# A written-out order of five engines set anew with every DMA landing counted, and one subtraction moved from GpSimd to VectorE

## The chip, the cores and the metric

The kernel runs on one core of one Trainium2 chip. The metric is the time of one execution on the device in microseconds, the median of several runs. The core has five engines with a queue of instructions each: TensorE (PE in the profile; its weight loads are PEld), VectorE (DVE), ScalarE (ACT), GpSimd (POOL) and SyncE (SP, which here only issues DMAs). An engine works its queue strictly in order; between engines there are semaphores.

## The reference

An attention block on 32 items, x and y (called ctx_2048) of 256 channels by 1024 columns each, all in fp32. Cut to its core:

```python
x_q = einsum('oc,bcn->bno', w_qk, y);  x_k = einsum('oc,bcn->bon', w_qk, x)
x_v = einsum('oc,bcn->bon', w_v, x) + b_v[None, :, None]
energy = einsum('bnc,bcm->bnm', x_q, x_k)               # 1024 x 1024
attention = softmax(energy, axis=-1)
attention = attention / (1e-07 + attention.sum(axis=1, keepdims=True))
x_r = einsum('bcn,bnm->bcm', x_v, attention)
return x + relu(einsum('oc,bcn->bon', w_t, x - x_r) + b_t[None, :, None])
```

## The kernel before

**Numbers.** Each fp32 operand of a matmul is kept as two fp32r forms, a high one (a rounded copy, made by ScalarE) and a low one (operand minus high form, made mostly by GpSimd). A product is three matmuls of 128x512: high by high, high by low, low by high. Products of 2x2 blocks are made with seven block products instead of eight (Strassen's scheme in Winograd's form), at the price of sums and differences of blocks on VectorE and GpSimd, and of reading partial results out of the banks.

**Words.** A word is one small step of one item, recorded on one engine. A table of words per stage of the program fixes the order: FIRST (item 0), STEADY (a loop body, run for items 1 to 29) and LAST. A plus in front of a word means the next item, a minus the one before. The function `do` goes through a table and calls each word; the class `InOrder` (line 62, the line that the profile gives for nearly everything) makes each of PE, DVE, ACT and POOL keep exactly this order. DMAs of SP are not in `InOrder`: their order among themselves is chosen by the framework that records the program. It also gives each DMA of SP one of eight semaphores in turn.

The words that matter here, for item b:

- `E0P1` to `E3P7`: products of the energies, four pairs of row tiles, accumulated in banks 0 to 3. `E.r.` (ACT) and `E.c..` (DVE) read and combine the banks; the latter also find the row minimum. `exp`, `ri` (reciprocal of the row sum), `h`, `l`, `sum`: exponential, high form, low form and column sums of a row tile.
- `A` + row tile, c, h: attention products, into banks 4 to 7 (c = 0: 4 and 5; c = 1: 6 and 7), with the value tiles `uf` as weights: row tiles 0 to 3 use the first half of `uf`, 4 to 7 the second.
- `xl0`, `xl1`: low forms of x, 512 and 1024 columns. `xT1` to `xT4` (POOL) are differences of x blocks, `xTh`, `xTl` their high and low forms. The same for y: `ys`, `yh`, `yl`, `ysh`, `ysl`.
- `uP`, `xP`, `kP`: products of x with folded weights: u (the values, turned), x (the part of the result without attention) and k (the keys). `kc`, `kT`, `kh`, `kl`, `kTh`, `kTl` make the key blocks and their forms (`kT3`, `kT2` and `kT4` on DVE, `kT1` on POOL).
- `ur`, `uc`: u out of the banks; `ud1` to `ud4` store it to `uspace` in DRAM; `ul0`, `ul1` (four DMAs each) load it back into `turned`; `ut` (DVE) turns it, `uh` (ACT) and `uL` (POOL) make its two forms in `uf`.
- `xr1` to `xr7` (ACT): x parts out of the banks; `xd` store them to `xspace` and `xmspace`. `xr5`, `xr6`, `xr7` write the buffers of `rs` that `ud4`, `ud2`, `ud3` read.
- The end of an item: `cols`, `inv`, `turn` (DVE: column sums, inverse), `div1`, `div0` (DVE: banks 6, 7 and banks 4, 5 into `z`), `join` (a DMA of POOL adds `xspace` to `z`), `more` (a DMA of POOL adds `xmspace`), `pos` (ACT: relu), `add` (a DMA of POOL adds x), `st` (SP stores the result). join, more, pos, add and st of one half of `z` each need the landing of the one before.
- `ldx`, `ldy`: loads of x and y, which share two buffers (`raws`).

So each period of STEADY holds work of three items, and PE has 81 products (243 matmuls) in it.

Of the kernel before, what the change touches and what calls it, by code (L numbers as in the profile page):

```python
# [17 lines left out]
def kernel(  # L18
# [900 lines left out]


    FIRST = """
        xh1 Fxh0 ys03 Fxl0 Fxl1 Sgram Swt Sgh0 ys01 Scorner ldy1 Stp ys02 Sbvw FHH0 Swtc
        FHL0 ys04 Ssq Sgraw Sgh1 Sgl Sbias yh00 yh01 Fyh Gh22 Svh FLH0 FHH1 Svl ysh0
        FLH1 FHL1 yh11 kh11 Fraw22 yl01 ysl0 kl11 kT3 kT2 ys11 yl00 Fyl Gl22 kT1 Gs1
        Fkh22 kh21 V01 V00 Fkl22 kl21 kT4 Fkh12 kTh0 FE10 Fkl12 yh10 Smraw Sth vh0 FE11
        FE00 FE01 Fmin1 vl0 kTh1 exp1 Th12 Ms3 Gs2 Stl kTl1 yl10 Gs3 Gs4 kTl0 yl11 ys12
        ri1 Ts3 ys13 ys14 V10 Fmin0 V11 Ts1 h11 sum11 h10 exp0 Ms1 l10 l11 FX00 Ts2 ri0
        E1P1 vh1 h01 FX01 vl1 sum01 l01 E1r1 Fxw00 h00 sum10 E1P6 E1P5 E1P7 FX11 Fxw01
        Gh12 Fxd00 +ldx0 sum00 l00 E1r2 Mh12 E1r3 E1c22 E1P4 Ml12 E1P2 E1P3 E1c21 ysh1
        +ldx1 ysl1 +xT3 +xT1 Gl12 Ts4 E1c11 exp3 E1c12 Fxw11 ri3 h31 exp2 sum30 sum31  # L930
        FX10 l31 A100 A111 A101 h30 E2P1 ri2 sum20 l30 h21 Th22 A011 E2r1 h20 GhS sum21
        l21 E2P6 E2P7 l20 E2r2 E2r3 +xh1 +xh0 E2P5 +xl0 E2P4 Mh22 E2c22 E2P2 ThS Ml22
        TlS E2P3 E2c21 +xT2 E2c11 E2c12 exp5 Fxw10 A000 A001 ri5 sum50 h51 A110 +xl1
        +ldy0 Fxd11 sum51 l51 Fxd10 exp4 A010 h50 A301 ri4 E3P1 sum41 l50 h40 l40 A200
        E3r1 h41 E3P6 l41 E3P7 E3P5 sum40 E3P2 E3r2 E3r3 +ys01 +xT4 E3P4 +xTh0 +xTh1 Ms2
        E3c22 E3c11 E3P3 E3c21 E3c12 A210 A300 exp7 +xTl1 exp6 ri7 A311 sum71 h71 ri6
        sum60 Ms4 A201 A211 A310 l71 h60 GlS +xTl0 Tl22 h70 l60 A410 +uP1 +uP2 +ldy1
        +ys11 +ys02 MhS Tl12 +ys03 +ur1 +ys12 MlS +uc1 +uP6 +yh01 h61 +ur2 +yh10 sum61
        l61 sum70 A510 l70 +uP7 +uP5 +ur3 +yh00 +uc3 +ud1 +uP4 +kP1 +uP3 +uc2 +yl00
        +ys13 A610 +ud2 +yh11 +kr1 +yl10 +yl01 +ys14 +ys04 +kP7 +ur4 +ysh0 +yl11 +ysl0  # L940
        +ud3 ++ldx0 +kP6 +ks2 +kP5 +ks3 +kP4 +kP2 +kc22 Fxd01 +ud4 +kc21 +kP3 +kc12 +kT3
        ++ldx1 +xP5 A701 +kh21 +xr6 +kT2 +kl21 +ul0 +kT4 +xP2 +xP3 +xP1 +ysh1 +xr5 +xr1
        ++xh0 A611 +xP6 A711 ++xl0 +kh11 +xr2 +kh22 +xr7 +kl11 +xP7 A511 +xr3 +xP4 A710
        +xd3 A411 +xr4 +xd2 +xd5 +xd6 +xd4 +xd1 +xd7
    """
    STEADY = """
        E0P1 kTh0 +xT3 kl22 kT1 kTl0 E0P2 +xh1 kTh1 kTl1 -A601 +xT1 E0r1 +xT2 E0P6 E0r2
        -cols ut0 E0P7 -inv -A501 E0r3 E0P5 -turn +xTh0 E0c22 -A700 E0P4 E0c21 E0c11
        -div1 -A500 exp1 ri1 -A600 -A401 -A400 +xT4 +xl1 E0P3 +uP1 +xTh1 -div0 h11 +xTl1
        l11 h10 sum10 +xTl0 E0c12 ysl1 sum11 l10 +ur1 exp0 +uP2 +xP1 +uc1 E1P1 E1P7 E1r1  # L950
        ri0 +uP6 sum00 E1P6 h01 +xP2 +uP5 sum01 l01 h00 E1r2 E1r3 l00 E1P5 E1c22 +ur2
        E1P4 uh0 +uP7 uL0 E1P2 +ldy1 +xr1 +ur3 +xP6 E1c21 +uP4 exp3 E1P3 E1c11 +uc3 +xr2
        +ud1 +ldy0 ri3 +ur4 sum31 +uP3 E1c12 -join0 +ys11 +ys12 ul1 h30 h31 A111 +ud3
        +xP7 exp2 A011 +uc2 l31 +xr3 +ud4 ri2 h21 E2P1 h20 E2r1 +xP5 l30 +ud2 sum30 +xP4
        sum21 E2P6 l21 E2P7 sum20 +yh01 +xr4 E2r2 +yh00 +xr5 +xr6 l20 E2P5 E2P2 E2r3
        E2P4 +xP3 +xr7 E2c22 E2c11 E2c21 E2P3 ut1 exp5 A100 ri5 A101 h51 E2c12 sum51 l51
        A110 A301 A000 A010 exp4 ri4 E3P1 h50 h40 E3r1 A001 sum41 l50 +ys01 +yl01 -join1
        +ys13 sum50 +ys14 +yl00 -more0 h41 sum40 +ys02 E3P6 l41 +ys03 E3P7 -more1 +ys04
        +yh10 E3r2 E3r3 A300 E3P5 l40 E3P4 E3c22 E3c21 E3P2 E3P3 A210 +xd2 +xd3 ++ldx0
        +xd1 +ysh0 A310 -pos1 uh1 uL1 +yl10 E3c11 E3c12 +yh11 A201 exp7 ri7 sum70 sum71  # L960
        A411 A311 A211 exp6 ri6 h70 +xd4 +ul0 -pos0 +xd6 +xd5 h71 +xd7 +yl11 sum61 l70
        sum60 h61 l71 A200 l61 h60 +kP1 +kr1 A511 ++xh0 +ysh1 +ysl0 +kP6 l60 +ks2 +kP7
        ++ldx1 +ks3 -add0 ++xl0 -add1 +kP5 +kP4 +kP2 +kc22 +kh11 +kc21 +kh21 +kP3 A510
        A701 A610 +kc12 +kT3 +kT2 +kl21 +kh22 +kT4 +kl11 A710 A410 -st0 -st1 A611 A711
    """
    LAST = """
        -E0P1 -ysl1 xh1 -kTh0 -kl22 -kT1 -kTh1 -kTl0 -E0r1 --cols -ut0 -kTl1 -E0P2 -E0P6
        -E0P7 --A501 -uh0 -E0r2 -E0P5 --inv -E0r3 -E0c11 -E0c22 -E0P4 --A700 --A601
        -E0P3 --A600 -E0c21 -exp1 --turn -ri1 -E0c12 --div1 -h11 xl1 xT1 -uL0 xT2 --A500
        -l11 -exp0 --A400 --A401 -ul1 -h10 uP1 -ri0 --div0 -h01 -h00 -sum11 -l10 xT4 xT3  # L970
        -sum10 uP2 -E1P1 ur1 -E1P7 -E1r1 -l01 -l00 -sum01 -sum00 --join0 -E1P6 -E1P5 uc1
        -E1P2 xTh1 -E1r2 -E1r3 xTl1 -A100 xTh0 -E1c22 xTl0 -E1P4 -E1c11 -E1c21 -A000 uP6
        -ut1 -E1P3 ldy0 ud1 -A110 -exp3 ur2 -ri3 uP7 uP5 -E1c12 -h31 -exp2 -sum30 -A010
        -sum31 -l31 --join1 ys01 ur3 uP4 -ri2 uc3 -h30 ys03 ys02 -E2P1 -sum20 -h21 ur4
        -E2r1 -l30 -l21 -sum21 uP3 uc2 -E2P6 --more1 ud4 -E2r2 -h20 ys04 --more0 -E2P7
        -A111 -E2P5 -E2r3 ldy1 -l20 -E2P4 -E2P2 ysh0 -A101 -uh1 -E2c22 -E2c21 -uL1 -E2P3
        -E2c11 -A301 -A001 -exp5 -ri5 -h51 -E2c12 -exp4 -sum50 -l51 ud2 -h50 -A201 -A310
        -A011 ud3 -sum51 ul0 -ri4 -l50 -sum40 -E3P1 yh00 -h41 -E3r1 -E3P7 -E3P6 -A211
        -h40 -E3r2 -sum41 -l41 --pos0 -l40 yh01 -E3P5 -E3r3 -E3P2 -E3c22 -E3P4 -E3P3
        -E3c11 yh11 -E3c21 -E3c12 ut0 -exp7 -exp6 -ri7 -sum71 -ri6 -A200 yl00 -sum70  # L980
        -A300 -A311 --pos1 -sum60 -A210 -A511 -A500 -A401 -A400 -A411 -h71 -h70 -l71
        -l70 -h61 -h60 -sum61 -l61 kP1 uh0 kP6 kr1 yh10 -l60 ysl0 --add1 kP7 ks2 kP5
        --add0 yl11 ks3 uL0 yl01 kP4 ul1 kP2 --st0 --st1 kc22 kc21 kh11 kP3 kc12 kh22
        kh21 kT3 kT2 kl21 -A410 -A701 kTh0 ys11 kT1 -A611 -A700 -A501 -A601 kT4 kl11
        kTl0 kTh1 E0P1 E0P2 E0r1 -A510 -cols -A610 E0P6 E0P7 -inv kTl1 E0r2 -turn E0P5
        E0r3 kl22 yl10 E0P4 E0c22 E0P3 E0c11 E0c21 -A600 E0c12 exp1 -div0 -A711 -A710
        exp0 ri1 -div1 xP1 h11 -join0 ri0 l11 h10 l10 -join1 h01 xP2 ys12 sum11 ys14 xr1
        sum10 E1P1 xP6 E1r1 E1P6 E1P7 l01 ut1 sum01 h00 xr5 -more1 -more0 E1P5 A100 ys13
        E1r2 ysh1 -pos1 -add1 l00 E1r3 sum00 E1P4 E1c22 -pos0 E1P2 E1c21 xr2 exp3 E1P3
        xP7 E1c11 xP5 -add0 xr3 E1c12 ri3 h31 A111 xP4 A000 sum30 exp2 xr6 l31 ysl1  # L990
        sum31 E2P1 h30 xr4 E2r1 ri2 sum21 xP3 xd5 xd2 xd3 h21 xd1 xd4 -st1 sum20 h20
        E2P6 l30 E2P7 l21 xd6 l20 E2P5 xr7 E2r2 E2P2 E2r3 E2P4 uh1 -st0 E2c22 E2c21 exp5
        E2c11 A101 E2P3 Zb1 E2c12 ri5 h51 exp4 Zx0 xd7 Zx1 A001 A110 sum50 sum51 l51
        A010 A011 E3P1 h50 ri4 A200 sum40 h41 l50 E3r1 l41 sum41 E3P6 E3P7 h40 E3r2 l40
        E3P5 E3r3 E3P4 E3P2 E3c22 E3c21 E3c11 E3P3 Zb0 E3c12 exp7 A210 Zc1 A300 A211
        A310 ri7 exp6 Zc0 uL1 A511 Zs1 sum71 sum70 ri6 h70 sum61 sum60 Zs0 l70 cols h60
        l60 inv A311 A710 A400 A410 A201 A600 A510 turn A610 A500 Zn1 Zn0 h61 A700 A301
        A501 A401 Zd10 Zm10 Zd00 h71 Za10 Zm00 l61 Za00 A411 l71 A611 A601 A711 A701
        Zd11 Zd01 Zt10 Zt00 Zm01 Zm11 Za01 Za11 Zt11 Zt01
# [46 lines left out]
```

## Time and profile before

| what | value |
|---|---|
| median of 3 runs | 1907.45 us (1899.95 to 1907.55) |
| the profiled execution, its own time | 1911.21 us |
| span of the profiled execution | 1909.4 us |
| mean granted TensorE clock | 0.996 |
| busy share PE / PEld / DVE / ACT / POOL | 96 / 76 / 88 / 77 / 76 % |
| DMA packets of SP's queue / of GpSimd's queue | 226.29 MB / 89.40 MB |

The page gives shares over the whole span; the loop makes nearly all of it. A busy PE there is not a PE at its peak, since matmuls overlap: what a matmul costs is read from the distance of starts in the order of time. A wait is put down to the engine whose semaphore came last.

### The profile page before, as it was taken

To read this page: it belongs to the slowest core of one execution; us is meant where nothing else is said; L and a number is where in the kernel's file an instruction comes from. 1 tells how busy PE (TensorE), PEld (TensorE's weight loads), DVE (VectorE), ACT (ScalarE), POOL (GpSimd) and SP (SyncE) were. 2 spreads that over 40 slices of the span, in tenths; PEclk is the share of its full clock that TensorE was granted. 3 is DMA by queue.
4 is the path that set the end of the run, shared out by engine and by line. 5 is a ranking of instruction groups with operands and counts; after the bars stand their busy time and mean duration, and the time that the engine had idled before them with its cause. 6 is when DMAs were issued, how large, how long until landed. Compare 5 with 4: busy or idle time off the path is not lost.

```text
span 1909.4 us, 26036 instructions
## 1 busy us (share of the span) xinstructions
PE 1840.0 (96%) x7843; PEld 1446.2 (76%) x7843; DVE 1686.2 (88%) x3209; ACT 1462.5 (77%) x2415; POOL 1449.4 (76%) x1163
## 2 busy tenths in 40 slices
...
GB/s 108 116 151 170 162 158 192 174 169 166 153 189 188 165 171 156 165 192 179 165 172 151 190 182 168 175 162 156 190 194 165 171 156 170 184 176 175 165 138 128
DMA packets 230621, 317.74 MB, mean 166 GB/s; under 512 B 16976, under 2 KB 144848, under 8 KB 230480
## 3 DMA queue, kind: packets, MB, share of 16 engines
q1 hardware_dynamic: 203280, 226.29, 35.2%
q0 software_dynamic: 26784, 89.40, 27.9%
...
## 4 chain that ended last, share of the span: by engine, by line
PE 58%; ACT 11%; DMA 11%; issue 10%; POOL 6%; DVE 3%; SPq 0%; POOLq 0%; DVEq 0%; ACTq 0%
PE banks L62 58%; DMA z<-xspace 6%; DMA uspace<-rs 4%; ACT banks L62 3%; ACT efs L62 3%; POOL uf L62 3%; ACT rs L62 3%; POOL sums L62 1%; ACT sums L62 1%; POOL yd L62 1%; DVE banks L62 1%; DVE acc L62 1%; DVE efs L62 0%; DVE z L62 0%; DMA turned<-in_ctx_dram 0%
## 5 line engine op out<-in xcount | busy, mean ns | idle before, releaser
L62 PE MATMUL banks<-efs,uf 128*128 128x512 f32 x3072 | 768.8, 391 | 29.9 <-POOL uf L62 28.3
L62 PEld LDWEIGHTS banks<-efs,uf 128*128 128x128 f32 x3072 | 575.1, 188 | 162.4 <-POOL uf L62 38.5
L62 PE MATMUL banks<-gf,ysum 128*128 128x512 f32 x1524 | 419.0, 397 | 0.8 <-ACT rs L62 0.7
L62 ACT COPY rs<-banks 128x512 f32<-128x512 f32 (+1 forms) x503 | 294.8, 593 | 143.0 <-PE banks L62 111.7
L62 DVE SCALAR_TENSOR_TENSOR efs<-banks,small,efs 128x512 fp32r<-128x512 f32 x512 | 373.3, 741 | 3.3 <-ACT efs L62 3.2
L62 ACT ACTIVATE efs<-banks,small 128x512 fp32r<-128x512 f32 x512 | 339.8, 700 | 30.6 <-PE banks L62 23.9
L62 PEld LDWEIGHTS banks<-gf,ysum 128*128 128x128 f32 x1524 | 278.4, 188 | 86.9 <-ACT rs L62 24.5
L62 DVE SCALAR_TENSOR_TENSOR acc<-banks,small,acc 128x512 f32<-128x512 f32 x448 | 329.1, 746 | 17.1 <-ACT efs L62 1.2
L62 PE MATMUL banks<-gf,yd 128*128 128x512 f32 x1158 | 316.1, 394 | 2.4 <-DVE small L62 1.5
L62 POOL TENSOR_TENSOR uf<-turned,uf 128x1024 fp32r<-128x1024 f32 x62 | 149.5, 2411 | 222.5 <-ACT uf L62 206.3
L62 ACT ACTIVATE banks<-banks,small 128x1024 f32<-128x1024 f32 x256 | 279.7, 1092 | 49.2 <-DVE small L62 49.0
L62 PEld LDWEIGHTS banks<-gf,yd 128*128 128x128 f32 x1158 | 212.3, 188 | 59.7 <-DVE rs L62 9.6
L62 POOL TENSOR_TENSOR sums<-raws 128x256 f32<-128x256 f32 (+1 forms) x188 | 223.3, 1188 | 0.0
L62 POOL TENSOR_TENSOR yd<-raws,yd 128x256 fp32r<-128x256 f32 x189 | 144.4, 790 | 95.9 <-ACT yd L62 94.1
L62 DVE TENSOR_TENSOR rs<-banks,rs 128x512 f32<-128x512 f32 x282 | 193.6, 686 | 22.9 <-PE banks L62 8.9
L62 DVE CUSTOM_DVE_ANT_0 banks<-banks,rs,small 128x512 f32<-128x512 f32 x254 | 191.7, 756 | 19.3 <-PE banks L62 5.6
L62 POOL TENSOR_TENSOR gf<-sums,gf 128x1024 fp32r<-128x1024 f32 (+1 forms) x95 | 193.6, 2056 | 16.7 <-ACT gf L62 16.7
L62 PE MATMUL banks<-xf,tws 128*128 128x512 f32 x651 | 184.7, 400 | 20.2 <-ACT sums L62 8.8
L62 PE MATMUL banks<-xf,mws 128*128 128x512 f32 x651 | 187.4, 397 | 2.5 <-DVE efs L62 1.2
L62 DVE CUSTOM_DVE_ANT_0 banks<-banks,rs 128x512 f32<-128x512 f32 x254 | 176.7, 706 | 13.9 <-PE banks L62 8.8
L62 PEld LDWEIGHTS banks<-xf,tws 128*128 128x128 f32 x651 | 120.5, 190 | 60.1 <-ACT rs L62 22.7
L62 PE MATMUL banks<-xf,gws 128*128 128x512 f32 x651 | 162.5, 396 | 0.3 <-DVE rs L62 0.2
...
## 6 DMA issues: line engine op xcount, KB each, us to landing
raws<-in_x_dram SPq DMA_DIRECT2D x66, 512.0 KB, 4.6
raws<-in_ctx_dram SPq DMA_DIRECT2D x124, 256.0 KB, 3.3
uspace<-rs SPq DMA_DIRECT2D x124, 256.0 KB, 5.7
...
z<-xspace POOLq DMA_DIRECT2D x62, 512.0 KB, 6.1
z<-in_x_dram POOLq DMA_DIRECT2D x62, 512.0 KB, 6.1
out_dram<-z SPq DMA_DIRECT2D x62, 512.0 KB, 3.8
xspace<-sums SPq DMA_DIRECT2D x120, 256.0 KB, 3.9
```

Source lines behind the costliest of these rows:

```text
L62: self.last = getattr(self.engine, name)(*args, **kwargs)
```

## The change

All three tables are written anew: the same words (but for where the tables meet) in another order. The planner behind them, which is not part of the kernel, now counts the landing of every DMA, those that GpSimd issues too. One instruction changes its engine: `xl1`, the low form of the second block of x (128x1024, both inputs in SBUF), goes from POOL to DVE.

```diff
     def x_low(b, k):
         to, v = x_own(b, k)
-        pool.tensor_tensor(to[:, LOW], v, value(to[:, HIGH]), ALU.subtract)
+        by = dve if k else pool
+        by.tensor_tensor(to[:, LOW], v, value(to[:, HIGH]), ALU.subtract)
...
     STEADY = """
-        E0P1 kTh0 +xT3 kl22 kT1 kTl0 E0P2 +xh1 kTh1 kTl1 -A601 +xT1 E0r1 +xT2 E0P6 E0r2
...
+        E0P1 kTh1 E0r1 E0P2 kTl1 ysh1 -A711 E0P6 E0r2 -inv ut0 uh0 E0P7 -turn E0r3 -A410
...
```

In the middle of a period, POOL before. The rows run from `join1` over `ys13`, `ys14`, `yl00`, `more0`, `ys02`, `ys03`, `more1`, `ys04` to `uL1`:

```order
L62 DMA z<-xspace 128x1024
L62 TENSOR_TENSOR sums<-raws 128x256
L62 TENSOR_TENSOR sums<-raws,sums 128x256
L62 TENSOR_TENSOR yd<-raws,yd 128x256
L62 DMA z<-xmspace 128x1024
L62 TENSOR_TENSOR sums<-sums,raws 128x256
L62 TENSOR_TENSOR sums<-raws 128x256
L62 DMA z<-xmspace 128x512
L62 TENSOR_TENSOR sums<-raws,sums 128x256
L62 TENSOR_TENSOR uf<-turned,uf 128x1024
```

POOL after, from `xTl0` and `xTl1` over `join0`, `uL0`, `ys01`, `ysl1`, `join1` and `more0` to `ys03`:

```order
L62 TENSOR_TENSOR xf<-sums,xf 128x1024 x2
L62 DMA z<-xspace 128x1024
L62 TENSOR_TENSOR uf<-turned,uf 128x1024
L62 TENSOR_TENSOR sums<-raws 128x256
L62 TENSOR_TENSOR ysum<-sums,ysum 128x1024
L62 DMA z<-xspace 128x1024
L62 DMA z<-xmspace 128x1024
L62 TENSOR_TENSOR sums<-raws 128x256
```

`join1` and `more0` now stand next to each other, ahead of all the y sums; `more1` comes seven rows behind `more0`, and `uL1` behind `add0`. On ACT, `pos0` moved from far behind `uh1` to between `xr6` and `xr5`, and `pos1`, which stood just ahead of `uh1`, to the period's end, behind the next x item's `xh0`.

At the head of a period, DVE before, from `turn` over the three block steps of E0 to `div1`, `ri1`, `div0` and `l11`:

```order
L62 STREAM_TRANSPOSE acc<-sc 128x1024
L62 ISA banks,small<-banks,rs 128x512
L62 ISA small 128x1
L62 ISA banks,small<-banks,rs,small 128x512
L62 ISA small 128x1
L62 ISA banks,small<-banks,rs 128x512
L62 ISA small 128x1
L62 SCALAR_TENSOR_TENSOR z<-banks,ubias,acc 128x1024
L62 RECIPROCAL small<-small 128x1
L62 SCALAR_TENSOR_TENSOR z<-banks,ubias,acc 128x1024
L62 SCALAR_TENSOR_TENSOR efs<-banks,small,efs 128x512
```

and after, from E0's last block step on:

```order
L62 ISA banks,small<-banks,rs,small 128x512
L62 ISA small 128x1
L62 SCALAR_TENSOR_TENSOR z<-banks,ubias,acc 128x1024
L62 RECIPROCAL small<-small 128x1
L62 TENSOR_TENSOR xf<-raws,xf 128x1024
L62 SCALAR_TENSOR_TENSOR z<-banks,ubias,acc 128x1024
L62 SCALAR_TENSOR_TENSOR efs<-banks,small,efs 128x512
```

The moved `xl1` stands between `ri1` and `div0`. `cols`, which stood behind the key steps, now stands among them, and `kc21` moved to behind `kc12`, so just ahead of `kT3` and `kT2`.

SP after, from `ldy` over the first DMA of `ul1`, `ud1`, the other three of `ul1`, `xd1`, then `ud4`, `ud2`, `ud3`, to the next `ldx0` and what follows it (before, `ud1` stood ahead of all four of `ul1`, `st0` and `st1` behind the second `ldx`):

```order
L211 DMA raws<-in_ctx_dram 128x4x128 x4
L503 DMA turned<-uspace 32x8x128
L498 DMA uspace<-rs 128x512
L503 DMA turned<-uspace 32x8x128 x3
L468 DMA xspace<-sums 128x512
L498 DMA uspace<-rs 128x512 x3
L468 DMA xspace<-sums 128x512 x2
L201 DMA raws<-in_x_dram 128x1024
L468 DMA xspace<-sums 128x512
L468 DMA xmspace<-rs 128x512 x3
L860 DMA out_dram<-z 128x1024
L503 DMA turned<-uspace 32x8x128 x4
```

`ud1` now waits in SP's queue behind a load into `turned`, which can start only when `uL0` has read the buffer.

More of the change, by code (lines that the diff above doesn't have):

```diff
@@ L921 @@
     FIRST = """
[L922 to L944, printed above, removed]
+        ys01 ys02 xh1 Sgram Sgh0 Scorner Sbvw Swt Stp yh01 Fxh0 Fxl1 Fxl0 ys03 ys04 Swtc
@@ new lines @@
+        FHH0 Ssq Sth Sgraw yh00 Sgh1 ysh0 FHL0 Smraw Sgl Svh FLH0 ldy1 +ldx0 Svl FHH1
+        FLH1 yh10 Sbias FHL1 Fkh12 Gh12 Fyh Fkh22 Th12 Fraw22 kh11 Th22 ysl0 V10 V11 V01
+        kT3 V00 yh11 kh21 yl10 ys11 Stl Gs1 yl01 Fyl ys13 Fkl12 kT2 yl11 kT4 kl11 kl21
+        Ms1 vh0 ys12 yl00 Gl12 FE10 Fkl22 kT1 vl0 FE11 Gh22 vh1 Fmin1 kTh0 kTl0 kTh1
+        ys14 Ts1 Ts2 vl1 FE01 FE00 FX11 FX01 exp1 Gs2 kTl1 ri1 Fmin0 +xT1 Ts3 h11 sum11
+        exp0 l11 sum10 E1P1 ri0 sum01 h10 E1r1 FX00 sum00 +ldx1 l10 E1P6 h01 E1P7 h00
```

117 lines of the change are left out of this document (67 added, 50 removed).

## The prediction

> **What bounds the kernel now.** I read the page first, then the chain that ended last, the waits, and one period in the order of time. In the chain the same releases come back every period:
>
> ```profile
> PE 1840.0 (96%) x7843; PEld 1446.2 (76%) x7843; DVE 1686.2 (88%) x3209; ACT 1462.5 (77%) x2415; POOL 1449.4 (76%) x1163
> ```
>
> ```profile
> 193.16 2.36 POOL uf L62
> ...
> 1241.58 2.40 POOL uf L62
> ...
> 1706.86 2.36 POOL uf L62
> ```
>
> `POOL uf` is `uL1`, once a period. Between the outer rows lie 26 periods: 1513.70 / 26 = 58.22 us. PE's rows of one period (start, duration):
>
> ```profile
> 1199.27 1.52 PE L62 MATMUL banks<-gf,yd 128*128 128x512 f32 x6
> 1226.97 1.65 PE L62 MATMUL banks<-gf,yd 128*128 128x512 f32 x6
> 1228.84 0.96 PE L62 MATMUL banks<-xf,tws 128*128 128x512 f32 x3 [0.23 <-ACT rs L62]
> 1240.87 2.65 PE L62 MATMUL banks<-efs,uf 128*128 128x512 f32 x11
> 1244.03 2.60 PE L62 MATMUL banks<-efs,uf 128*128 128x512 f32 x10 [0.50 <-POOL uf L62]
> 1252.08 4.92 PE L62 MATMUL banks<-efs,uf 128*128 128x512 f32 x21
> 1256.84 1.52 PE L62 MATMUL banks<-gf,yd 128*128 128x512 f32 x6
> ```
>
> From 1252.08 to 1256.84 run 21 matmuls, 0.2267 us each, so 0.68 a product and 243 x 0.2267 = 55.1 us a period. PE thus loses 3.1 us a period, whatever the 96% say. At two places by these rows: ahead of `xP3` (1228.84 - 1226.97 - 6 x 0.2267 = 0.5) and in `A411` (1244.03 - 1240.87 - 11 x 0.2267 = 0.7). Over the span:
>
> ```profile
> POOL uf L62 <- ACT uf L62: 206.3, 28, 9.3
> PE banks L62 <- POOL uf L62: 28.3, 24, 1.7
> PE banks L62 <- ACT sums L62: 8.8, 1, 8.8
> ```
>
> The 28.3 us in 24 waits are 1.2 each (up to 1.7). I put `A411` at 1.3 and `xP3` at 0.6 a period, the remaining 1.2 at small waits of 0.1 to 0.2.
>
> Why `A411` waits: POOL's own rows, with t = 0 at 1199.27, the period's first product.
>
> ```profile
> 1197.06 1.30 POOL L62 TENSOR_TENSOR sums<-sums 128x512 f32<-128x512 f32 x1
> 1207.04 2.41 POOL L62 TENSOR_TENSOR xf<-raws,xf 128x1024 fp32r<-128x1024 f32 x1
> 1209.42 4.75 POOL L62 TENSOR_TENSOR xf<-sums,xf 128x1024 fp32r<-128x1024 f32 x2
> 1218.84 0.85 POOL L62 DMA_DIRECT2D z<-xspace  x1
> 1227.62 0.88 POOL L62 DMA_DIRECT2D z<-xspace  x1 [1.04 <-issue]
> 1230.30 1.18 POOL L62 DMA_DIRECT2D z<-xmspace  x1
> 1241.58 2.39 POOL L62 TENSOR_TENSOR uf<-turned,uf 128x1024 fp32r<-128x1024 f32 x1 [6.77 <-ACT uf L62]
> ```
>
> ```profile
> 1239.51 1.06 ACT L62 ACTIVATE z<-z 128x1024 f32<-128x1024 f32 x1 [1.02 <-DMA z<-xmspace]
> 1240.47 1.03 ACT L62 CAST uf<-turned 128x1024 fp32r<-128x1024 f32 x1
> ```
>
> `join1` at t = 28.4 makes `more1` late, `pos1` waits on ACT for its landing, `uh1` stands behind `pos1`, `uL1` behind `uh1`, PE behind `uL1`: one chain of three in-order queues.
>
> **The change, part by part.**
>
> *uL1.* After, no `pos` stands ahead of `uh1` but `pos0`, some ten ACT steps earlier. `uh1` follows E3's first read, so about t = 36 to 37.5, `uL1` ends 1 + 2.4 us later, near 41. Its first user, `A401`, is PE's 65th product: 64 x 0.68 = 43.6 and the small waits. The 1.3 us go.
>
> *xl1 on DVE.* POOL is relieved of 2.41 us, DVE takes 1.2. That price holds only if the two engines do not meet:
>
> ```profile
> 9.01 1.23 DVE L62 TENSOR_TENSOR xf<-raws,xf 128x1024 fp32r<-128x1024 f32 x1 [0.83 <-ACT xf L62]
> 25.99 2.40 POOL L62 TENSOR_TENSOR gf<-sums,gf 128x1024 fp32r<-128x1024 f32 x1
> 26.94 1.60 DVE L62 TENSOR_TENSOR z<-rs 128x128 f32<-128x128 f32 x1
> 64.07 2.39 POOL L62 TENSOR_TENSOR xf<-sums,xf 128x1024 fp32r<-128x1024 f32 x1
> 64.94 1.68 DVE L62 TENSOR_TENSOR z<-rs,z 128x128 f32<-128x128 f32 x1
> ```
>
> A DVE subtraction of 128x128 with both inputs in SBUF took 1.60 and 1.68 us, more than the 1.23 of one eight times its size; both ended 0.15 us after the POOL instruction that was running (25.99 + 2.40 and 64.07 + 2.39). So such a DVE instruction waits for POOL's. `xl1` is the first of its kind in the loop. Where does it fall? DVE's rows:
>
> ```profile
> 1195.44 1.48 DVE L62 TENSOR_TENSOR sums<-banks,sums 128x512 f32<-128x512 f32 x2
> 1198.62 1.23 DVE L62 TRANSPOSE_TENSOR_REDUCE parts<-acc 128x32 f32<-128x1024 f32 x1
> 1208.31 1.28 DVE L62 SCALAR_TENSOR_TENSOR z<-banks,ubias,acc 128x1024 f32<-128x1024 f32 x1
> ```
>
> `kT2` ends at 1196.92. `div0` starts 11.4 us later, of which `cols` (1.2), now earlier, drops out: `xl1` takes its place 10.2 after `kT2`. POOL starts `kT1` at 1197.06, right after `kT2`, and reaches the old place of `xl1` at 1207.04, 10.1 after `kT2`; there `xTl0` now stands. A dead heat, and POOL works without a gap there. `kc21`, now ahead of `kT3`, makes both 0.6 later: t = 8.4.
>
> If POOL is first, `xl1` waits for `xTl0` (2.4), ends near 12, and `div0` ends at 13.2. `uP5`, PE's 17th product, due at 16 x 0.68 + 0.2 = 11.1, needs `div0`: PE waits 2.1. If DVE is first, PE waits nothing here, and POOL waits between 0 (no row shows a POOL instruction waiting for DVE) and the whole 1.2. I take 1.2: the rows show that the two exclude each other.
>
> [...]
>
> *The DMAs of POOL.* POOL after: `xTl0`, `xTl1` (4.75) and the 1.2 from t = 8.4: `join0` at 14.3 (before 1218.84 - 1199.27 = 19.6). Then 0.6 for its issue, `uL0` 2.4, `ys01` 0.7, `ysl1` 2.4: `join1` at 20.4 (before 28.4), `more0` at 21.0 (before 31.0). What it means for their landings, and for SP's stores beside them, from the DMAs issued in three stretches of this period, 1212 to 1213, 1218 to 1225 and 1227.5 to 1232 (last number: us from issue to landing):
>
> ```profile
> uspace<-rs SPq DMA_DIRECT2D x1, 256.0 KB, 2.1
> ```
>
> ```profile
> uspace<-rs SPq DMA_DIRECT2D x3, 256.0 KB, 4.8
> z<-xspace POOLq DMA_DIRECT2D x1, 512.0 KB, 6.1
> ```
>
> ```profile
> z<-xspace POOLq DMA_DIRECT2D x1, 512.0 KB, 5.3
> z<-xmspace POOLq DMA_DIRECT2D x1, 512.0 KB, 5.6
> ```
>
> A store to `uspace` alone lands in 2.1 us, behind a `join` in 4.8: I read that as landing after it. After, `ud4`, `ud2` and `ud3` are issued at t = 22 to 24, behind `join1` and `more0`. `join1` lands at 20.4 + 6.0 = 26.4. `more0` landed 3.0 behind `join1` here (1230.30 + 5.6 against 1227.62 + 5.3); issued only 0.6 behind it, I take the same 3.0 (bounds: 0.6, and 5.6 if the two do not overlap): 29.4. `ud2` then lands near 30, `xr6` ends at 30.6. `xP3`, the 43rd product, is due at 42 x 0.68 + 0.3 = 28.9 where DVE won, and waits 1.8; where POOL won it is due at 31.0 and waits nothing. So the two cases end alike: about 2 us lost ahead of `xP3`, once by `xl1`, once by the DMAs.
>
> `ud1`, behind the first `ul1` DMA, which waits for `uL0` (17.3), lands behind `join0` near 21; `ur4`, its user, is due at 20.2 (DVE first) or 22.3: up to 0.3 at `A111`.
>
> *The rest.* The order of the energy products and their reads is the same but for a place or two; every buffer I followed is free 0.1 to 0.5 us ahead of its next user, as before. I cost it at nothing; its cover is DVE, 88% busy, so any lag of DVE shows. `ldx1` is issued near t = 46, its user `xT3` stands at 52. FIRST: zero, within 4 either way.
>
> *LAST.* There PE stands once for 9 us:
>
> ```profile
> 1853.35 6.94 DMA z<-xmspace
> ```
>
> The 8.8 of `ACT sums` above is this place: ACT stands at `pos1` and `pos0` with `xr2` behind. After, `div1` and `div0` come ahead of E0, `join` near t = 2, `more` lands near 15 to 18, while ACT wants `pos1` at 14. A stall of 3 to 4 remains: a gain of 5.
>
> **The sum.** Period after = 55.1 + 1.2 small + 2.0 less 0.3 (the small wait that `div0` makes already) = 58.0 where POOL wins; 55.1 + 1.2 + 1.8 + 0.3, less 0.7 that a `more0` landing early may spare = 57.7 where DVE wins. I take 57.85: 0.37 x 29 periods = 10.7 us. With 5 from LAST 16 us: 1911.2 becomes 1895 for a profiled execution. The median of the runs stands 3.8 below that execution: 1907.45 - 16 = 1891.5.
>
> **The rivals.**
>
> *The order pays in full.* `xl1` meets a gap and the stores land in time: only small waits stay, 55.1 + 1.2 = 56.3; 1.9 x 29 + 5 = 60: 1847. For it: at nearly every place the new order is as tight as the old one and not tighter. Against it: POOL has no gap where `xl1` falls. [...]
>
> *One wait for another.* The loss ahead of `xP3` is 2.4 instead of 2.0: 58.2, as before; LAST alone counts: 1902. That the planner's landings change nothing on the chip is this case too.
>
> *Slower.* `pos0` now stands between `xr6` and `xr5` on ACT and waits for `more0`. If two POOL transfers issued 0.6 us apart do not overlap, `more0` lands at 26.4 + 5.6 = 32.0, `pos0` ends at 33.0, `xr5` at 33.6; `A100` needs it and is due at 32.5 where POOL won: 1.1 more, 59.1 a period, 0.9 x 29 - 5 = 21 slower: 1928. It decides from a landing of `more0` at t = 31 on. For it: no pair in the rows stands that close. Against it: `join1` and `more0`, 2.7 apart here, finish without a POOL wait between them.
>
> **How the numbers follow.** A run tells 0.5% (9.5 us) from no change. My forecast has 0.5 (its own range 1880 to 1902), full pay 0.17, one wait for another 0.18, slower 0.15. Faster: 0.85 of the first and all of the second, 0.60; same: the rest of the first and nearly all of the third, 0.24; slower 0.16. The range reaches from 1850, most of full pay, to 1918, the slow edge of no change.
>
> **What would show it.** `POOL uf <- ACT uf` short of PE's notice and no `PE <- POOL uf`; `DVE xf<-raws,xf` with a mean near 3.6 us (POOL first) or POOL's `xf<-sums,xf` with one of 3.6 (DVE first), against 1.2 and 2.4; PE waiting for `DVE z` or for `ACT rs`; `z<-xmspace` landing 8 us after its issue. If `xl1` takes 1.2 and the stores land in 3, I am wrong on the low side; if ACT waits for `z<-xmspace`, on the high side.

## The result, and the profile after

The changed kernel takes 1951.17 us (median of 4 runs, 1949.37 to 1958.09) against 1906.12 for the kernel before on the same chip: a ratio of 1.025, 95% interval 1.0215 to 1.0284. It is slower, outside the range of the prediction (1850 to 1918). The profiled execution took 1949.8 us for a span of 1948.0. The page after, first two lines:

```profile
span 1948.0 us, 26013 instructions
PE 1850.0 (95%) x7843; PEld 1461.6 (75%) x7843; DVE 1779.5 (91%) x3240; ACT 1474.5 (76%) x2415; POOL 1407.6 (72%) x1132
```

The period is read from PE's first product `E0P1` of the first and of the 29th steady period (start, duration):

```profile
90.72 1.66 PE L62 MATMUL banks<-gf,yd 128*128 128x512 f32 x6
...
1765.24 1.52 PE L62 MATMUL banks<-gf,yd 128*128 128x512 f32 x6
```

1674.52 / 28 = 59.80 us, against 58.24 before by the same two products (91.3 and 1722.1). What comes ahead of the first row is 0.6 us shorter than before, what comes behind the second 182.8 in place of 187.3. So the loss is in the loop: 1.56 us in each of 28 periods, 43.7, less those 5. Who makes PE wait, over the span (us, times, longest):

```profile
POOL uf L62 <- PE banks L62: 186.5, 29, 8.9
PE banks L62 <- DVE z L62: 53.8, 30, 1.9
ACT rs L62 <- DMA uspace<-rs: 41.0, 22, 3.9
PE banks L62 <- ACT rs L62: 24.2, 19, 3.0
```

Before there were 28.3 us for `POOL uf` in this list; now `uL1` waits for PE's notice and PE never for `uL1`. In their place stand two new waits: 1.8 in every period for DVE's `z` (`div0`), and in 19 of them for ACT's `rs` (`xr6`), which itself waits for a store to `uspace`. The chain of waits holds both; one period of it, in order of time:

```profile
1233.12 0.09 DVE xf L62
1233.21 3.24 issue
1236.45 1.28 DVE z L62
...
1237.87 6.50 PE banks L62 x27
...
1248.33 0.56 DVE rs L62
1248.90 7.26 DMA uspace<-rs
1256.18 0.59 ACT rs L62
...
1256.82 10.24 PE banks L62 x42
```

The first stretch is `xl1`: 3.24 us in which DVE has begun it and nothing that the profile shows holds it. The same place in the order of time, with POOL beside it, then the groups over the span (busy us, mean ns of one):

```profile
1233.04 5.71 POOL L62 TENSOR_TENSOR xf<-sums,xf 128x1024 fp32r<-128x1024 f32 x2
1233.12 3.40 DVE L62 TENSOR_TENSOR xf<-raws,xf 128x1024 fp32r<-128x1024 f32 x1
1237.87 1.38 PE L62 MATMUL banks<-xf,mws 128*128 128x512 f32 x5 [1.88 <-DVE z L62]
```

```profile
L62 POOL TENSOR_TENSOR xf<-sums,xf 128x1024 fp32r<-128x1024 f32 x62 | 175.2, 2848 | 1.5 <-ACT xf L62 1.5
L62 DVE TENSOR_TENSOR xf<-raws,xf 128x1024 fp32r<-128x1024 f32 x32 | 102.2, 3193 | 2.1 <-ACT xf L62 2.1
```

`xTl0` starts 0.08 us ahead of `xl1`. `xl1` takes 3.40 in place of 1.23, and of POOL's two instructions, 2.4 each alone, the second takes 3.35, so it waits for the part of `xl1` that ran behind the first. Below, "the lock" is this, as these rows show it: `xl1`, a DVE instruction with two inputs in SBUF, and a POOL instruction that reads SBUF hold each other up (3.40 in place of 1.23, 3.35 in place of 2.4).

The second stretch: the DMAs issued from 1243 to 1246.1 (t = 18.2 to 21.3; t = 0 at 1224.82), and the three stores from 1246 to 1250.5 (last number: us from issue to landing):

```profile
z<-xspace POOLq DMA_DIRECT2D x1, 512.0 KB, 7.2
z<-xmspace POOLq DMA_DIRECT2D x1, 512.0 KB, 9.4
```

```profile
uspace<-rs SPq DMA_DIRECT2D x3, 256.0 KB, 7.4
```

Before, `join1` and `more0` took 5.3 and 5.6, and the three stores 4.8. A third loss is in neither list. Another period, PE's rows, and the granted clock by stretch (columns: us, busy PE, PEld, DVE, ACT, POOL with counts, PEclk, DMA share, GB/s):

```profile
1000.05 2.38 PE L62 MATMUL banks<-xf,mws 128*128 128x512 f32 x6 [1.86 <-DVE z L62]
1002.23 1.48 PE L62 MATMUL banks<-gf,yd 128*128 128x512 f32 x3
1003.51 1.12 PE L62 MATMUL banks<-gf,ysum 128*128 128x512 f32 x3
```

```profile
998.00:1000.00 2.00, 0.19 (x1) 0.00 (x0) 2.00 (x3) 0.11 (x2) 2.00 (x1) 1.00 0.00 0
1000.00:1002.00 2.00, 1.95 (x6) 1.60 (x7) 1.89 (x4) 1.96 (x3) 2.00 (x3) 0.66 0.82 236
1002.00:1004.00 2.00, 2.00 (x7) 1.52 (x6) 1.50 (x3) 0.78 (x3) 2.00 (x2) 0.50 0.70 113
1004.00:1006.00 2.00, 2.00 (x10) 1.67 (x9) 1.06 (x3) 1.98 (x4) 2.00 (x3) 0.98 1.01 204
```

Behind the wait of 1.86 the product that starts at 1002.23 takes 1.28 us to the next start (1003.51 - 1002.23) in place of 0.68: 0.43 a matmul in place of 0.227, and the granted clock of that stretch is 0.50. In the 25 middle periods 85 matmuls start 0.41 to 0.45 us after the one before them (2 in the kernel before). At 0.2 us each that is 17.0 us, 0.68 a period.

So the period after is 55.1 of pure matmuls, 2.0 ahead of `uP5`, 0.9 ahead of `xP3` (a mean; up to 3.2), 0.7 at half rate, and 1.1 of small waits: 59.8.

### The profile page after: what moved, and what is told of

Read it like the earlier page. It is cut to its first block, busy times and chain, and to the rows that moved or that the text cites. A ratio compares the mean times of both kernels' runs of the same rounds, so it can differ in the third digit from the quotient of the medians.

```text
span 1948.0 us, 26013 instructions
## 1 busy us (share of the span) xinstructions
PE 1850.0 (95%) x7843; PEld 1461.6 (75%) x7843; DVE 1779.5 (91%) x3240; ACT 1474.5 (76%) x2415; POOL 1407.6 (72%) x1132
## 4 chain that ended last, share of the span: by engine, by line
PE 37%; DVE 29%; DMA 10%; issue 10%; POOL 9%; ACT 4%; DVEq 0%; POOLq 0%; SPq 0%; ACTq 0%
PE banks L62 37%; DVE banks L62 8%; DMA uspace<-rs 7%; POOL gf L62 5%; DVE acc L62 5%; DVE efs L62 4%; POOL sums L62 3%; DVE rs L62 3%; DMA raws<-in_ctx_dram 3%; DVE sums L62 2%; DVE parts L62 2%; DVE z L62 2%; ACT banks L62 1%; DVE small L62 1%; ACT gf L62 1%
## 5 line engine op out<-in xcount | busy, mean ns | idle before, releaser
L62 PE MATMUL banks<-gf,ysum 128*128 128x512 f32 x1524 | 426.0, 401 | 0.6 <-ACT rs L62 0.3
L62 ACT ACTIVATE efs<-banks,small 128x512 fp32r<-128x512 f32 x512 | 343.2, 699 | 36.2 <-PE banks L62 28.3
L62 PEld LDWEIGHTS banks<-gf,ysum 128*128 128x128 f32 x1524 | 280.8, 190 | 91.3 <-ACT rs L62 22.1
L62 POOL TENSOR_TENSOR uf<-turned,uf 128x1024 fp32r<-128x1024 f32 x62 | 158.1, 2550 | 186.8 <-PE banks L62 186.5
L62 PEld LDWEIGHTS banks<-gf,yd 128*128 128x128 f32 x1158 | 216.2, 191 | 63.1 <-DVE efs L62 8.2
L62 POOL TENSOR_TENSOR sums<-raws 128x256 f32<-128x256 f32 (+1 forms) x188 | 207.9, 1106 | 3.8 <-DMA raws<-in_ctx_dram 3.8
L62 PE MATMUL banks<-xf,tws 128*128 128x512 f32 x651 | 184.2, 399 | 24.0 <-ACT rs L62 22.4
L62 PEld LDWEIGHTS banks<-xf,mws 128*128 128x128 f32 x651 | 123.1, 194 | 94.2 <-issue 64.6
L62 POOL TENSOR_TENSOR xf<-sums,xf 128x1024 fp32r<-128x1024 f32 x62 | 175.2, 2848 | 1.5 <-ACT xf L62 1.5
```

The costliest lines, as they stand in the source:

```text
L62: self.last = getattr(self.engine, name)(*args, **kwargs)
```

## The experiments

Losses per period, as means over 25 middle periods from the starts of PE's products (us), with the period and the time of the runs. "uP2, uP5" is the wait for `div0` (with the order alone, `xl1` first and all three, for POOL's `xf`), "xP3" the one for `ud2`, "half rate" the matmuls at 0.43. Period and losses are of the profiled execution, which was up to 10 us longer than the median (1929.5 against 1919.5 with `more0` and `pos0` late, 1946.4 against 1937.0 with the engine alone); that is 0.3 a period:

| kernel | period | uP2, uP5 | xP3 | other | half rate | median | ratio to before |
|---|---|---|---|---|---|---|---|
| before | 58.24 | 0.2 | 0.6 | A411 1.3 | 0.0 | 1906 | 1 |
| changed | 59.80 | 2.0 | 0.9 | | 0.7 | 1951 | 1.025 |
| order alone | 61.95 | 1.2 | 3.1 | | 1.2 | 2009 | 1.054 |
| engine alone | 59.27 | 1.2 | 0.5 | A411 1.4 | 0.2 | 1937 | 1.016 |
| one input | 59.37 | 0 | 2.6 | | 0.7 | 1942 | 1.017 |
| more0 late | 61.06 | 2.0 | 0 | A100 1.7 | 1.3 | 1990 | 1.044 |
| more0, pos0 late | 58.83 | 2.0 | 0 | E3P1 0.3 | 0.3 | 1919 | 1.006 |
| xl1 first | 60.68 | 0.5 | 2.8 | | 1.1 | 1980 | 1.037 |
| all three | 57.72 | 0.5 | 0.2 | E3P1 0.8 | 0.0 | 1892 | 0.990 |
| before, uh1 first | 57.31 | 0.2 | 0.6 | kP1 0.5 | 0.0 | 1887 | 0.988 |

**The order alone.** The changed tables, `xl1` on POOL again:

```diff
-        by = dve if k else pool
-        by.tensor_tensor(to[:, LOW], v, value(to[:, HIGH]), ALU.subtract)
+        pool.tensor_tensor(to[:, LOW], v, value(to[:, HIGH]), ALU.subtract)
```

> The changed kernel's three orders, with xl1 back on POOL, where it stands between xTl0 and xTl1. Theory (xl1 on DVE is what costs, by the lock between a two-input DVE instruction and POOL): the 2.0 us that PE waits ahead of uP5 in each period fall to 0.3 or less, DVE's groups have no 3.2 us row, POOL's xf<-sums,xf is back at 2.4 us. POOL gets to join0 about 1.2 us later than in the changed kernel (t = 15.1 against 13.9), join1 and more0 too, so the wait ahead of xP3 stays at 1 to 3: period 57.5 to 59.0, time 1885 to 1930. Rival (the new order is what costs, whichever engine has xl1, because join1 and more0 stand ahead of the stores ud2 to ud4): the loss ahead of xP3 takes up all that uP5 gives back, period 59.5 to 60.5, time 1940 to 1970.

Measured: 2009.23, ratio 1.0538 (1.0505 to 1.0571), slower than either theory said. Its waits:

```profile
ACT rs L62 <- DMA uspace<-rs: 113.1, 40, 4.9
PE banks L62 <- ACT rs L62: 85.2, 35, 4.0
PE banks L62 <- POOL xf L62: 26.4, 29, 0.9
```

No wait for DVE's `z`, as the lock has it, and POOL's group is back at 2.41. But `join1` and `more0` come at t = 21.3 and 21.9 (19.9 and 20.5 in the changed kernel), `ud2` lands at 33.4 in place of 31.4, and PE waits 3.1 for it and 1.2, inside `uP2`, for POOL's `xTl1`; 1.2 more go at half rate. The rival's mechanism was right, its size too small, since it counted neither the wait for `xTl1` nor the half rate. So the new order costs 103 us with `xl1` on POOL, and on this order the move to DVE gains 58.

**The engine alone.** The old tables, `xl1` on DVE (the first diff the other way round).

> The three orders of the kernel before, with xl1 on DVE, where it stands between ri1 and div0. Theory (lock): POOL stands idle for xTh1 there, so xl1 meets no POOL instruction in most periods and takes about 1.2 to 1.3 us; div0 comes 1.2 later, which PE sees as a wait of about 1 us ahead of uP2 or uP5; POOL, 2.4 us shorter ahead of join0, brings join1, more1 and uL1 forward, so that the 1.3 us in A411 shrink or go: period 57.5 to 58.7, time 1885 to 1920. Rival (DVE is full, and any 1.2 us more on it cost the period as much, without a lock): period 59.2 to 59.6, time 1930 to 1945, with the waits spread over DVE's small reads.

Measured: 1937.02, ratio 1.016 (1.012 to 1.0201). DVE is first here, by 0.5 us, in the order of time:

```profile
1221.89 1.21 DVE L62 TENSOR_TENSOR xf<-raws,xf 128x1024 fp32r<-128x1024 f32 x1
1222.37 2.96 POOL L62 TENSOR_TENSOR xf<-sums,xf 128x1024 fp32r<-128x1024 f32 x1 [1.57 <-ACT xf L62]
```

`xl1` takes 1.21, and this time it is POOL's instruction that takes longer, 2.96 in place of 2.41. `div0` ends 1.0 later and PE loses 1.2 ahead of `uP2`, as expected. But POOL did not bring `join0` forward: it stood idle for ACT's `xf` instead, 1.57 us here, was held 0.55 by the lock, and `join0` came at 20.3 (19.6 before). So `A411` waits as before. The time is in the rival's range, but its waits are not spread, they stand at one place. The move alone costs 31 us, the order alone 103, both together 45.

**One input.** The changed kernel, with `xl1` on DVE reading x only:

```diff
-        by.tensor_tensor(to[:, LOW], v, value(to[:, HIGH]), ALU.subtract)
+            dve.tensor_reduce(to[:, LOW], v.unsqueeze(2), AX.X, ALU.max)
```

> The changed kernel, with the second block's xl1 on DVE as an instruction with one input of the same size (a maximum over an axis of length one, so the second low form is a copy of x and no longer the remainder). Theory (lock): it takes 1.1 to 1.3 us in place of 3.19 and does not wait for POOL, POOL's xf<-sums,xf falls from 2.85 to 2.4, the wait ahead of uP5 falls from 2.0 to 0.3 or less, join0 comes 0.9 earlier; what is lost ahead of xP3 stays or grows, since xP3 is then due 2 us earlier while the stores land only 0.5 to 1 earlier: 1.5 to 2.5. Period 58.0 to 59.2, time 1895 to 1930. Rival (not the lock but DVE's full queue): the instruction is 1.2 but uP5 still waits 1 to 2 us, period 59 to 59.8, time 1925 to 1951.

Measured: 1941.50, ratio 1.0169 (1.0123 to 1.0214). The two groups, and the wait:

```profile
L62 DVE TENSOR_REDUCE xf<-raws 128x1024 fp32r<-128x1024 f32 x31 | 37.7, 1218 | 0.0
...
L62 POOL TENSOR_TENSOR xf<-sums,xf 128x1024 fp32r<-128x1024 f32 x62 | 148.3, 2414 | 2.0 <-ACT xf L62 2.0
```

```profile
PE banks L62 <- ACT rs L62: 70.2, 30, 3.6
```

1.22 in place of 3.19, POOL 2.41 in place of 2.85, nothing ahead of `uP5`: the lock is shown, and a DVE that is merely longer by 1.2 us costs nothing here. But the period falls by 0.43 alone. PE reaches `xP3` 2 us earlier, `ud2` lands at 31.1 (31.4), so the wait there grows from 0.9 to 2.6, a little more than expected. With the half rate, which the theory did not count, the time lies above its 1930 and in the rival's range, but the rival's wait ahead of `uP5` is not there.

**more0 late.** The changed kernel, `more0` moved on POOL (the words as in the table):

```diff
-        h30 E1c12 +uc2 sum31 +xP7 uL0 +ys01 ysl1 -join1 -more0 +ys03 exp2 ul1 l31 +xr3
+        h30 E1c12 +uc2 sum31 +xP7 uL0 +ys01 ysl1 -join1 +ys03 exp2 ul1 l31 +xr3
...
-        +ys12 +ys14 +yl01 -more1 +xr6 E2c22 +xP3 E2c21 -pos0 E2c11 ut1 +xr5 E2P3 +xr7
+        +ys12 +ys14 -more0 +yl01 -more1 +xr6 E2c22 +xP3 E2c21 -pos0 E2c11 ut1 +xr5 E2P3 +xr7
```

> The changed kernel, with more0 moved in the steady order from behind join1 to behind ys14, some 6 us later on POOL. Theory (the stores ud4, ud2, ud3 land behind join1 and more0, which together take 9.9 us): ud2 lands at t = 27 to 28 in place of 31.4, the 0.9 us ahead of xP3 go, those ahead of uP5 (2.0, the lock) stay: period 58.8 to 59.2, time 1920 to 1935. Rival 1 (join1 alone delays the stores, or xP3 waits for something else): ud2 still lands beyond 30, period as in the changed kernel, 59.8, time 1951. Rival 2: more0 now lands too late for pos0, which stalls ACT ahead of xr5 and PE ahead of A100: period 60 or more, time 1955 to 1980.

Measured: 1990.48, ratio 1.0441 (1.0408 to 1.0475). The theory's mechanism and rival 2 both came, and the time is above either range. `more0` is issued at 25.6 in place of 20.5, `ud2` lands at 29.2 (27 to 28 expected) in place of 31.4, 4.1 us after its issue in place of 7.0, and nothing is lost ahead of `xP3`. But `more0` lands at 33.4, ACT stands at `pos0`, and `xr5` and `A100` stand behind it:

```profile
1282.41 1.06 ACT L62 ACTIVATE z<-z 128x1024 f32<-128x1024 f32 x1 [1.62 <-DMA z<-xmspace]
1283.38 1.05 ACT L62 COPY rs<-banks 128x512 f32<-128x512 f32 x2
...
1284.00 4.17 PE L62 MATMUL banks<-efs,uf 128*128 128x512 f32 x17 [0.76 <-ACT rs L62]
```

**more0 and pos0 late.** As that one, with `pos0` behind `exp5` on ACT:

```diff
-        ... +xP3 E2c21 -pos0 E2c11 ut1 +xr5 E2P3 +xr7
-        A100 A101 A001 A000 exp5 ri5 h51 ...
+        ... +xP3 E2c21 E2c11 ut1 +xr5 E2P3 +xr7
+        A100 A101 A001 A000 exp5 -pos0 ri5 h51 ...
```

> The kernel with more0 late, with pos0 moved too, from ahead of xr5 to behind exp5 on ACT, some six ACT steps later. Theory (the loss of that kernel ahead of A100, 1.7 us and 0.9 behind it at half the matmul rate, is ACT standing at pos0 for more0's landing at t = 33.4): both go, nothing is lost ahead of xP3, and what stays is the 2.0 us ahead of uP5 (the lock) with 0.6 behind it and 0.8 of small waits: period 58.5 to 58.9, time 1910 to 1930. Rival (landings that come later at join and more hold up something else as soon as ACT no longer waits, add0 or the next period's buffers): a new wait of 1 us or more, period 59.5 or more, time 1945 or more.

Measured: 1919.45, ratio 1.0058 (1.0036 to 1.008); the period is 58.83. As expected, the lock's wait is left, and 0.3 ahead of `E3P1`:

```profile
PE banks L62 <- DVE z L62: 53.9, 30, 1.9
...
PE banks L62 <- ACT rs L62: 1.8, 2, 1.5
```

**xl1 first.** The changed kernel with two neighbours on DVE exchanged:

```diff
-        -A701 +xT4 +xTl0 -A500 +xTh1 +uP1 ri1 +xl1 E0P3 ...
+        -A701 +xT4 +xTl0 -A500 +xTh1 +uP1 +xl1 ri1 E0P3 ...
```

> The changed kernel with xl1 and ri1 exchanged on DVE: xl1 comes 0.16 us earlier, at t = 8.14, ahead of POOL's xTl0 at 8.22 to 8.24, which it lost to by 0.08 us. Theory (the two engines exclude each other, and whichever starts second waits): DVE's xl1 takes 1.2 to 1.3 us in place of 3.2, POOL's xTl0 takes 3.4 to 3.6 (the group's mean 2.9 to 3.0), the wait ahead of uP5 falls from 2.0 to 0.3 or less, join0 comes at t = 14.0 to 14.3; xP3 is then due 2 us earlier with the stores no earlier, so 2.5 to 3.2 are lost there: period 59.0 to 59.7, time 1925 to 1947. Rival (only DVE waits for POOL and never the other way): POOL's group mean 2.4, join0 at 12.9 to 13.1, as in the kernel with the one-input instruction: period 59.2 to 59.5. Rival 2 (POOL's claim is made when its instruction is queued, not when it starts): nothing changes, xl1 3.2, 1951.

Measured: 1979.78, ratio 1.0372 (1.0342 to 1.0402), slower than the changed kernel by 29 us. The race is turned round:

```profile
1252.43 1.34 DVE L62 TENSOR_TENSOR xf<-raws,xf 128x1024 fp32r<-128x1024 f32 x1
1252.65 5.75 POOL L62 TENSOR_TENSOR xf<-sums,xf 128x1024 fp32r<-128x1024 f32 x2
```

`xl1` takes 1.34, POOL's `xTl0` 3.39 and `xTl1` 2.41 (medians over the periods), `div0` ends 2.3 earlier, and `join0` comes at 13.9, as in the changed kernel. So the lock works both ways in these runs, and POOL loses 1 us whoever is first (3.35 and 3.39 in place of 2.4). The stores are now issued 1.7 earlier, at 21.5 to 22.9, but `ud2` lands at 32.0, 0.7 later, since `more0` takes 11.1 in place of 9.9. PE waits 2.8 for it, and the half rate costs 1.1 in place of 0.7: 0.9 worse in all, where 0.1 to 0.8 better was expected: the wait at `xP3` came as forecast, the half rate behind it was not in the sum.

**All three.** `xl1` ahead of `ri1`, `more0` behind `ys14`, `pos0` behind `exp5`.

> All three edits at once: xl1 ahead of ri1, more0 behind ys14, pos0 behind exp5. Theory (the lock ahead of uP5 and the stores behind more0 ahead of xP3 are the whole loss): ud2 lands at t = 28.5 to 29.5, xP3, due at 29, waits 0 to 0.5, uP5 nothing, no matmuls at half rate; period 56.5 to 57.2, time 1855 to 1878, so faster than the kernel before. Rival (a join1 that lands later or the y sums that more0 now stands behind take up the gain): period 57.6 to 58.4, time 1885 to 1910, within 1% of the kernel before.

Measured: 1891.83, ratio 0.9903 (0.9888 to 0.9918): faster than before. The waits for `div0` and for `ud2` are gone, and with them the half rate (2 such matmuls in 25 periods):

```profile
PE banks L62 <- DVE small L62: 19.3, 29, 1.5
...
PE banks L62 <- ACT rs L62: 5.3, 10, 2.1
```

The period is 57.72 in place of 56.5 to 57.2, and so is in the rival's range, because a new wait of 0.8 has come ahead of `E3P1`: `pos0` now stands ahead of `exp4` on ACT.

**pos0 later still.** Behind `E3r1` in place of `exp5`, else as the last.

> The kernel with all three edits, with pos0 one step later still on ACT: from behind exp5 to behind E3r1. Theory (the 0.83 us that PE loses there ahead of E3P1 are pos0's 1.06 us on ACT ahead of exp4): they go, period 57.72 to 56.9 to 57.1, time 1866 to 1878. Rival (pos0 there makes uh1 and add0 late, so that uL1 or st0 holds up A401 or the next join): period 57.5 or more, time 1885 or more.

Measured: 1891.20, ratio 0.9905 (0.9879 to 0.9932): no change. The wait ahead of `E3P1` went and one of 0.5 ahead of `E3P4`, with some 0.1 at `E3P2` and at `xP3`, came. The rival's time held, but neither `uL1` nor `st0` is what is late; that DVE is next behind by half a microsecond, I had not seen.

**div0 later, without the lock.** The engine-alone kernel with two one-input instructions for `xl1`:

```diff
-        by.tensor_tensor(to[:, LOW], v, value(to[:, HIGH]), ALU.subtract)
+            for _ in range(2):
+                dve.tensor_reduce(to[:, LOW], v.unsqueeze(2), AX.X, ALU.max)
```

> The orders of the kernel before with xl1 on DVE as two one-input instructions in a row (each 1.22 us; the second block's low form is a copy of x), so that no lock plays a part and div0 ends 1.2 us later than in the kernel with only the engine changed: PE waits 2.3 to 2.5 ahead of uP2 in place of 1.19. [...] Period 59.3 to 60.3. Rival (the half rate of the changed kernel has to do with its DMAs, full in that stretch, not with the wait): no matmul at 0.43 us, period 58.9 to 59.4.

Measured in one execution: 2014.96, period 61.37. PE's rows, and the clock by stretch:

```profile
1274.46 0.97 PE L62 MATMUL banks<-xf,mws 128*128 128x512 f32 x3 [2.26 <-DVE z L62]
1275.27 1.42 PE L62 MATMUL banks<-xf,tws 128*128 128x512 f32 x3
1276.49 1.48 PE L62 MATMUL banks<-gf,yd 128*128 128x512 f32 x3
```

```profile
1271.00:1274.40 3.40, 1.21 (x6) 0.67 (x4) 3.37 (x4) 1.33 (x3) 3.16 (x2) 1.00 0.00 0
...
1275.20:1278.00 2.80, 2.80 (x8) 2.18 (x8) 2.35 (x6) 2.17 (x4) 2.80 (x2) 0.52 0.59 181
```

The wait is 2.4 in every period, and behind it matmuls run at 0.43 us in 19 of 25; with 13 behind waits in `A411` they are 149 in all, 1.2 us a period. With the same order of DMAs and a wait of 1.2 (the engine alone) there were 29, 24 of them in `A411`; and in the changed kernel the stretch from 1004, with a DMA share of 1.01, had a granted clock of 0.98. So in these runs the half rate follows PE's wait and not the DMAs. The period is a microsecond above the range expected. That range has 0.4 to 0.8 a period for the half rate, an estimate that no run shows for this wait; 1.2 came. And `A411` still waits 0.9, because `uL1`'s chain is later too.

**Before, with uh1 first.** One exchange in the old steady order:

```diff
-        +xd1 +ysh0 A310 -pos1 uh1 uL1 +yl10 ...
+        +xd1 +ysh0 A310 uh1 uL1 -pos1 +yl10 ...
```

> The kernel before with one exchange in its steady order: uh1 ahead of pos1 on ACT (uL1 with it), nothing else. Theory (A411's wait there is the chain more1, pos1, uh1, uL1): the 1.26 us a period go, period 58.24 to 57.0, 29 times 1.25 = 36 us: time 1865 to 1878. Rival (uL1 is as late without pos1, because uh1 waits for its data, or pos1, now later, holds up add1 and st1 in turn): 1895 to 1915, no change.

Measured: 1887.47, ratio 0.9881 (0.9863 to 0.99): 22.4 us below the kernel before on that chip, not 36. The 1.26 us in `A411` are gone, so the chain by `pos1` is shown; 0.5 of them came back at once ahead of `kP1`, where PE waits for DVE's `efs`, and the wait for ACT's `sums` in LAST grew from 8.8 to 10.5.

**The end too.** That kernel, with `pos1`, `pos0`, `add1`, `add0` behind `xr4` in LAST:

```diff
-        E1r2 ysh1 -pos1 -add1 l00 E1r3 sum00 E1P4 E1c22 -pos0 E1P2 E1c21 xr2 exp3 E1P3
-        xP7 E1c11 xP5 -add0 xr3 E1c12 ...
-        sum31 E2P1 h30 xr4 E2r1 ri2 ...
+        E1r2 ysh1 l00 E1r3 sum00 E1P4 E1c22 E1P2 E1c21 xr2 exp3 E1P3
+        xP7 E1c11 xP5 xr3 E1c12 ...
+        sum31 E2P1 h30 xr4 -pos1 -pos0 -add1 -add0 E2r1 ri2 ...
```

> The kernel before with uh1 ahead of pos1 and, in its last order, both pos and add steps moved from among E1's steps to behind xr4, where the changed kernel has them. Theory (the 10.5 us for which PE there waits for ACT's sums is ACT standing at pos1 and pos0 for more's landing, as read for the prediction's 5 us): 7 to 10 us go, time 1877 to 1881 where the one exchange alone gave 1887. Rival (the end is then set by the stores behind add1 and add0 instead): 1885 to 1890.

Measured: 1881.85, ratio 0.9859 (0.9833 to 0.9886), the fastest of all, 5.6 us below the last. The one wait at the end, first in the last kernel and then in this one:

```profile
1837.91 2.93 PE L62 MATMUL banks<-xf,tws 128*128 128x512 f32 x6 [10.52 <-ACT sums L62]
```

```profile
1830.98 2.93 PE L62 MATMUL banks<-xf,tws 128*128 128x512 f32 x6 [3.72 <-ACT sums L62]
...
1859.96 14.37 PE L62 MATMUL banks<-efs,uf 128*128 128x512 f32 x55 [2.05 <-POOL uf L62]
```

6.8 us of it go (7 to 10 expected). A wait of 2.05 for `uL1`, now behind `add1` and `add0` on POOL, takes some back; the span is only 2.5 shorter.

## Why the prediction was wrong, point by point

- *What bounds the kernel.* Right: PE with 55.1 us of matmuls, and two places where it waits. The chain behind the larger one, by `pos1`, is shown by the kernel before with `uh1` first.
- *uL1.* Right: PE waits for it nowhere after.
- *xl1 on DVE.* Right in mechanism and size. POOL won by 0.08 us; `xl1` ended at t = 11.7 (12 in the prediction), `div0` at 12.9 (13.2), `uP5` waited 2.0 (2.1). With DVE first, POOL lost 1.0 (1.2). That 1.2 was an estimate: the rows of the kernel before showed only DVE behind POOL. The runs show both directions: DVE 3.40 against 1.23 behind POOL, POOL 3.39 against 2.41 behind DVE; and the DVE instruction with one SBUF input, 1.22, was not held.
- *The DMAs of POOL: the step that failed.* "where POOL won it is due at 31.0 and waits nothing. So the two cases end alike": they do not, the two losses add up. PE came to `xP3` as late as forecast, but `more0` took 9.9 us and not 8.4, landed at 30.4 (29.4), and `ud2` at 31.4 (30): 0.9 us a period, where the two estimates together had left PE a reserve of only 0.4. In the other case, `xl1` first, the wait was 2.8 and not 1.8, for the same reason. I had spaced `more0` behind `join1` by a pair that ran almost alone: from 1229 to 1234 of the kernel before, POOL's queue moved 219 packets and SP's 1. In the changed kernel both stand among SP's transfers, and `join1` took 7.4 in place of 6.0. That is not the work of `more0`, since `join1` took 7.7 with `more0` issued 5.7 us behind it; in 1245 to 1246, right behind its issue, SP's queue moved 472 packets and POOL's none, so loads of `ul1` ahead of it are the likely cause, which no run moved alone. That `more0` holds up the stores is shown by the kernel with `more0` late (`ud2` 4.1 us after its issue in place of 7.0). How POOL's queue and SP's share the DMA engines stays open: the traces show 83 packets of POOL's queue and 73 of SP's from 1251 to 1253, but 85 and 12 in the kernel before from 1221 to 1223, with SP's loads and stores issued.
- *Left out of the sum.* A wait of PE was priced at its own length. But matmuls at half rate (0.43 us) can come behind it, in 26 of 77 waits of 1.9 to 2.1 us (the table at the end), in the changed kernel 0.7 a period. The kernel before has waits of up to 1.9 in `A411`, but only 2 such matmuls in 25 periods, so nothing in its rows gave the price.
- *The sum.* 58.0 for the case that came; 59.8 measured. The 1.8 are 0.9 at `xP3`, 0.7 at half rate, and 0.2 at small waits (the 0.3 that I subtracted for `div0` were not to be had). Times 28 that is 50 us, nearly all of the 55 between the 1895 forecast for a profiled execution and its 1949.8.
- *LAST and FIRST.* Right in size: 4.5 and 0.6 gained, 5 and 0 forecast. The stall of 3 to 4 that was to remain in LAST did not: of the 8.8 for ACT's `sums` 0.9 stayed, and waits for DVE's `efs` grew from 0.5 to 3.2, so that the size is partly luck.
- *The rivals.* The rival on the slow side, with `pos0` behind `more0`, did not happen in the changed kernel (`more0` landed at 30.4, its point was 31), but it was real: with `more0` at 33.4 it cost 1.7 us at `A100`. The full pay had neither of its conditions: `xl1` met POOL's instruction, and the stores came late. "One wait for another" was the nearest in mechanism, with both waits counted instead of one.

That the two losses together make the result is shown: taking the lock's wait alone away (one input, `xl1` first) changed the period by -0.4 and +0.9, taking the stores' wait alone away (`more0` and `pos0` late) by -1.0, both together by -2.1.

Open: why `more0` took 11.1 us in the kernel with `xl1` first and 9.9 in the changed one, though issued at the same time; the stores that came 1.7 us earlier beside it are the likely cause, but no run moved them alone.
